# Layer 0 of a two-layer transformer: ScalarE in the order of the source, later sums of the experts' weights, and their last step as a stream of its own

## The chip, the cores and the metric

The kernel runs on one core of a Trainium2 chip. The metric is the device time of one execution in microseconds (us); the time of a kernel is the median of several executions. The engines are TensorE (PE: matmuls, with PEld its weight loads), VectorE (DVE), ScalarE (ACT), GpSimd (POOL) and SyncE (SP, which here only issues DMAs).

## The reference, cut to what matters

Two layers, each of attention and a feed-forward part, each with a layer norm ahead of it and added to a residual, on 4 sequences of 512 rows of width 256. All is in float32.

```python
x = x + _L0_attn_ref(_layernorm(x), w_project, w_out)      # 16 heads of 16, causal, softmax over keys
x = x + _L0_ffn_ref(_layernorm(x), router_w, router_b, expert_w, expert_b)
x = x + _L1_attn_ref(_layernorm(x), w_qkv, w_proj)
x = x + _L1_ffn_ref(_layernorm(x), gate..., up..., down...)  # 4-bit weights

# _L0_ffn_ref: for every row and every one of 256 outputs a router over 8 experts
logits = (h @ router_w.T + router_b).reshape(T, O, E)
probs = softmax(logits, axis=-1)
w, sel = top_k(probs, 2)
w = w / sum(w, axis=-1)
c = zeros((T, E)).at[t_idx, sel].add(w)          # an expert's weights summed over the outputs
expert_out = einsum('th,eoh->teo', h, expert_w) + expert_b
final = einsum('te,teo->to', c, expert_out)
```

So each row has 256 x 8 logits; from each eight the two greatest are taken, their normalised weights are `sigmoid` of their gap and one minus it, and for each of the 8 experts these are summed over the 256 outputs. The change lies in how and when these sums are made.

## The kernel before

The residual stays in SBUF as 16 row tiles of 128 rows (`xres`), in 4 blocks of 4 tiles. Layer 0's attention runs over 44 batches (`batches`): a block j, a sequence s, and one to four groups of heads. For batch n the loop does, in this order:

1. `greatest(n + 1)`: first scores of the next batch (L631), in four PSUM tiles of the pool `l0_sc`, which has five; `shift(n)`: a transpose of the maxima (L660) and their subtraction from the queries by VectorE (L663); `mask(n + 1)` (L644), and VectorE's maxima of the first scores (L650, four operations).
2. A fill: pieces of other work, up to a budget of TensorE and VectorE time.
3. `mixed(n - 1)`: powers times values (L715, copied by ScalarE at L723); `powers(n)`: second scores (L679) in four tiles of the same five, then four exps on ScalarE (L688) and a causal select on POOL (L698).
4. A second fill.

As first and second scores share five PSUM banks, `powers(n)` needs banks that the maxima of batch n + 1 have read, and `greatest(n + 2)` needs banks that the exps of batch n have read.

What a fill gives out is cut into pieces by generators, each in a `Stream`: a piece tells which engine's budget it takes, how much, after how many slots, and on what condition. A slot is one call of `fill`; outside the waiting loops at a block's end there are two in a batch. The streams are asked in the order of the list `streams`. Layer 0's feed-forward part runs wholly in such streams, about half of it in the fills of layer 1's attention (`between`):

- `logit_pieces`: router products (L226, `lg_ps`), copied by ScalarE to `lg` (L289); tile g is allowed when `g - 2 in weights`.
- `weight_pieces`: for each row tile, on VectorE, the two greatest of eight (L363 to L378), then `lesser` on ScalarE (a tanh, L382, and L383, deferred by two slots), the logits less the second greatest (L389), and for each expert two accumulations. One is on VectorE (`junk`, L413). The other is `sum_up` on ScalarE (L406): the sum of `relu(-owing)` over the outputs, where `owing` is a running VectorE tile (L400, L416). Last, two small operations (L419, L420) turn sums into weights `c1`, and `weights[g]` tells that they are there.
- `result_pieces`: expert products (L226, `eo`), scaled by ScalarE with `c1` (L315, `part`); `addition_pieces` adds them to the residual (L342 to L344).
- `made()` counts the steps of `weight_pieces`, 17 for each tile, and paces products.

An operation put off with `defer` is issued at the start of the first fill that is at least one slot later (or as many as asked):

```python
for due in [d for d in deferred if d[0] <= slot]:
    deferred.remove(due)
    due[1]()
```

The projections of the attention's next block (`project`) are copied by ScalarE to `stage`, a tile with one buffer (L533); eight DMAs issued by SP (L539) spread each half to `qk`, and the copy for the next half waits for them to land. All products of a fill, and the transposes and outputs of `divided` (`av_T`, `oq_T`, whose copy `aT` is L753, and `o`, L762), share the PSUM pool `dn` with two buffers.

The order of the instructions on an engine is either that of the source, for the engines named in `manual_schedule`, or chosen by the framework when the program is built, with operations under `high_priority` preferred. In layer 0 TensorE, VectorE and POOL are in the order of the source and ScalarE is not; layer 1 adds ScalarE.

Of the kernel before, what the change touches and what calls it, by code (L numbers as in the profile page):

```python
# [8 lines left out]
F32 = mybir.dt.float32  # L9
# [3 lines left out]
ALU = mybir.AluOpType  # L13
# [3 lines left out]
P = 128  # L17
HID = 256
NS, NB = 4, 512
NT = 16  # L20
# [5 lines left out]
NE = 8  # L26
# [6 lines left out]
def tile_transformer(  # L33
# [19 lines left out]
    nc = tc.nc  # L53
# [11 lines left out]
    for t, eng in ((0, nc.sync), (2, nc.scalar)):  # L65
        eng.dma_start(out=xres[:, t : t + 2, :], in_=x[:, t : t + 2, :])
    in_order = ctx.enter_context(ExitStack())
    order = {mybir.EngineType.PE, mybir.EngineType.DVE, mybir.EngineType.Pool}
    in_order.enter_context(tc.manual_schedule(engines=order))
    ident = const.tile([P, P], F32, name="ident")  # L70
    make_identity(nc, ident)
# [26 lines left out]
    w_ffn0 = ctx.enter_context(ExitStack())  # L98
# [2 lines left out]
    ew = wa.tile([P, 2, NE, HID], F32, name="ew")  # L101
    b1 = w_ffn0.enter_context(tc.tile_pool(name="f0_1", bufs=1, side="right"))
    b2 = w_ffn0.enter_context(tc.tile_pool(name="f0_2", bufs=2, side="right"))
    b5 = w_ffn0.enter_context(tc.tile_pool(name="f0_5", bufs=5, side="right"))

# [1 line left out]
    slot = 0  # L109

    def need(engine, cost, gap=0, cond=None):
        return engine, cost, gap, cond
# [18 lines left out]
    streams = []  # L131
    deferred = []

    def defer(emit, slots=1):

        deferred.append((slot + slots, emit))

    left = {"PE": 0.0, "DVE": 0.0}

    def fill(**budget):  # L140

        nonlocal slot
        slot += 1
        for due in [d for d in deferred if d[0] <= slot]:
            deferred.remove(due)
            due[1]()
        for engine, b in budget.items():
            left[engine] = min(left[engine], 0.0) + b
        again = True
        while again:  # L150
            again = False
            for stream in list(streams):
                while stream.ready(left):
                    engine, cost = stream.go()
                    left[engine] -= cost
                    again = True
                if stream.next is None:
                    streams.remove(stream)

    normed = []  # L160

# [91 lines left out]
    logits, weights, halves = {}, {}, {}  # L253
# [20 lines left out]
    def logit_pieces():  # L274

        nonlocal products_left
        for g in range(NT):
            for pair in range(4):
                yield need(
                    "PE", 1.85,  # L280
                    cond=lambda g=g, pair=pair, at=(g - 0.9 + 0.22 * pair if g > 1 else 0.0):
                    g // 4 in xTs and (0, pair) in folded and (g < 2 or g - 2 in weights) and made() >= at,
                )
                if not pair:
                    lg = b2.tile([P, NE, HID], F32, tag="lg", name=f"lg{g}")
                ps = ps_dn.tile([P, 512], F32, tag="dn", name=f"lg_ps{g}_{pair}")
                dense(ps, g, rw, pair)
                products_left -= 1
                nc.scalar.copy(  # L289
                    lg[:, 2 * pair : 2 * pair + 2, :].rearrange("p e o -> p (e o)"), ps  # L290
                )
            logits[g] = lg, slot
# [32 lines left out]
    def counted(pieces):  # L325
        nonlocal steps_made
        for piece in pieces:
            yield piece
            steps_made += 1
# [3 lines left out]
    def addition_pieces():  # L333
        for g in range(NT):
            for half in range(2):
                yield need(
                    "DVE", 1.55,
                    cond=lambda k=(g, half): k in halves and halves[k][1] < slot,
                )
                part = halves[g, half][0]  # L340
                tt = nc.vector.tensor_tensor
                tt(part[:, 0:2], part[:, 0:2], part[:, 2:4], ALU.add)  # L342
                tt(part[:, 0], part[:, 0], part[:, 1], ALU.add)
                tt(xres[:, g, :], xres[:, g, :], part[:, 0], ALU.add)  # L344
                added[g, half] = slot

    def weight_pieces():

        tt, stt = nc.vector.tensor_tensor, nc.vector.scalar_tensor_tensor
        lessers = []  # L350
        for g in range(NT):
            yield need("DVE", 1.25, cond=lambda: g in logits and logits[g][1] < slot)
            d = logits[g][0]
            hi4 = b1.tile([P, 4, HID], F32, tag="hi4", name=f"hi4_{g}")
            lo4 = b1.tile([P, 4, HID], F32, tag="lo4", name=f"lo4_{g}")
            m2 = b1.tile([P, HID], F32, tag="m2", name=f"m2_{g}")
            gap = b1.tile([P, HID], F32, tag="gap", name=f"gap_{g}")
            th = b1.tile([P, HID], F32, tag="th", name=f"th_{g}")
            w1 = b1.tile([P, HID], F32, tag="w1", name=f"w1_{g}")
            c1 = b2.tile([P, NE], F32, tag="c1", name=f"c1_{g}")  # L360
            sums = b2.tile([P, NE + 1], F32, tag="sums", name=f"sums_{g}")

            tt(hi4, d[:, 0:4], d[:, 4:8], ALU.max)  # L363
            yield need("DVE", 1.25)
            tt(lo4, d[:, 0:4], d[:, 4:8], ALU.min)
            yield need("DVE", 1.4)
            lo2, hi2 = lo4[:, 0:2], lo4[:, 2:4]
            tt(lo2, lo2, lo4[:, 2:4], ALU.max)
            tt(hi2, hi4[:, 0:2], hi4[:, 2:4], ALU.max)
            yield need("DVE", 1.4)  # L370
            tt(hi4[:, 0:2], hi4[:, 0:2], hi4[:, 2:4], ALU.min)
            tt(lo2, lo2, hi4[:, 0:2], ALU.max)
            yield need("DVE", 1.7)
            tt(gap, hi2[:, 0], hi2[:, 1], ALU.min)
            tt(m2, lo2[:, 0], lo2[:, 1], ALU.max)
            tt(m2, m2, gap, ALU.max)
            tt(gap, hi2[:, 0], hi2[:, 1], ALU.max)
            tt(gap, gap, m2, ALU.subtract)  # L378


            def lesser(th=th, gap=gap, w1=w1):
                nc.scalar.activation(th, gap, AF.Tanh, scale=0.5)  # L382
                nc.scalar.activation(w1, th, AF.Identity, bias=half_t, scale=0.5)  # L383
                lessers.append(th)

            defer(lesser, 2)
            for e in (0, 4):
                yield need("DVE", 1.25)
                tt(  # L389
                    d[:, e : e + 4], d[:, e : e + 4],  # L390
                    m2.unsqueeze(1).to_broadcast([P, 4, HID]), ALU.subtract,
                )

            yield need("DVE", 0.7, 1, cond=lambda: lessers)
            lessers.clear()
            owing = b5.tile([P, HID], F32, tag="owing", name=f"owing_{g}_")
            nc.vector.tensor_scalar(gap, gap, 0.0, -1.0, ALU.is_equal, ALU.mult)
            stt(owing, th, -1.0, gap, ALU.add, ALU.add)  # L400
            nc.vector.memset(sums[:, NE : NE + 1], 0.0)
            for e in range(NE):

                def sum_up(e=e, owing=owing, sums=sums, g=g):
                    spare = b2.tile([P, HID], BF16, tag="spare", name=f"spare_{g}_{e}")
                    nc.scalar.activation(  # L406
                        spare, owing, AF.Relu, scale=-1.0, accum_out=sums[:, e : e + 1]
                    )

                defer(sum_up)  # L410
                yield need("DVE", 0.95, cond=lambda: len(deferred) < 4)
                junk = b2.tile([P, HID], BF16, tag="junk", name=f"junk_{g}_{e}")
                stt(junk, d[:, e], 0.0, w1, ALU.is_gt, ALU.mult, accum_out=c1[:, e : e + 1])  # L413
                if e < NE - 1:
                    less = b5.tile([P, HID], F32, tag="owing", name=f"owing_{g}_{e}")
                    stt(less, d[:, e], 0.0, owing, ALU.is_equal, ALU.add)  # L416
                    owing = less
            yield need("DVE", 0.3, 1)
            tt(sums[:, :NE], sums[:, :NE], sums[:, 1:], ALU.subtract)  # L419
            stt(c1, sums[:, :NE], 0.5, c1, ALU.mult, ALU.add)  # L420
            weights[g] = c1, slot
            del logits[g]

    normed_first = []

# [7 lines left out]
    with ExitStack() as l0:  # L433
# [293 lines left out]
        def divided(j, s):  # L727
# [29 lines left out]
            for t in (0, 2):  # L757
# [12 lines left out]
                    yield need("DVE", 0.7, 1)  # L770
                both = xres[:, 4 * j + t : 4 * j + t + 2, :]
                nc.vector.tensor_tensor(both, both, ps, ALU.add)
            fold_at = streams.index(fold) if fold in streams else len(streams) - 4
            streams.insert(fold_at if j else 0, Stream(hidden_pieces(j)))


# [24 lines left out]
        for piece in inputs_T(1, both[1][0], xT):  # L801
# [4 lines left out]
        done = blanked = 0  # L806
        fold = Stream(fold_pieces())
        streams += [
            inputs[1], fold, Stream(addition_pieces()), Stream(counted(weight_pieces())),
            Stream(result_pieces()), Stream(logit_pieces()),  # L810
        ]
        for n in range(NBT):
            j, s, gs = batches[n]
# [90 lines left out]


    with ExitStack() as l1:
        in_order.enter_context(tc.manual_schedule(engines={mybir.EngineType.Activation}))
        wb = l1.enter_context(tc.tile_pool(name="w_l1", bufs=1))
        wqkv = wb.tile([P, 2, NKV, HPK + 2, P], F32, name="wqkv")

# [376 lines left out]
```

## Time and profile before

| what | value |
|---|---|
| median of 3 executions | 1183.99 us (1183.14 to 1185.19) |
| the profiled execution | 1185.96 us, of which the span 1184.2 us |
| mean granted clock of TensorE | 0.995 of full speed |
| TensorE busy | 1153.4 us, 97% of the span |
| VectorE busy | 807.9 us, 68% |
| ScalarE busy | 485.2 us, 41% |
| POOL busy | 106.4 us, 9% |
| layer 0's attention | to about 400 us of the span |
| last expert product of layer 0's feed-forward part | at 738 us, in layer 1's attention |

How to read the views: a row of a timeline has the start, the duration, the engine, the line of the kernel, the operation, what it writes and reads, the shape, and how many instructions were merged (`x4`); in brackets stand the idle time of the engine ahead of it and what ended that. A row of the waits has who waited, for whom, the microseconds in total, how often, and the longest. A row of the windows has a stretch of the span, its length, the busy time of PE, PEld, DVE, ACT and POOL with their numbers of instructions, the granted clock, the DMA share and GB/s.

### The profile page before, as it was taken

What the parts mean: (1) busy time and instruction counts of PE and PEld (TensorE: products, weight loads), DVE (VectorE), ACT (ScalarE), POOL (GpSimd) and SP (SyncE); (2) the same over time, 40 slices, a digit from 0 to 9 for tenths busy, and PEclk for the clock granted to TensorE, in tenths of its full rate; (3) what the DMA queues carried; (4) which work ended last, traced back from release to release, by engine and by line L of the source; (5) the groups of instructions that cost most, each with busy time, mean ns of one, the idle gap of its engine ahead of it and who ended that gap; (6) DMA issues with size and microseconds to landing.
All of it is one profiled execution on the core that took longest, in us unless ns stands there. A gap on an engine that the chain in (4) does not pass through costs nothing.

```text
span 1184.2 us, 18603 instructions
## 1 busy us (share of the span) xinstructions
PE 1153.4 (97%) x7178; PEld 666.0 (56%) x7178; DVE 807.9 (68%) x1783; ACT 485.2 (41%) x1099; POOL 106.4 (9%) x152
## 2 busy tenths in 40 slices
PE   7999999999999899999999999999999999999998
PEld 3666555555555445555555556566644465475487
DVE  5676779889889777368646783888599844725710
ACT  1434545555466444445344542455244322303300
POOL 7322112112111000000000000000000000000000
PEclk9999999999999999999999999999999999999999
DMA  7230010000000310000000001021010000000000
GB/s 216 66 79 2 16 22 1 2 1 1 2 1 2 117 62 1 1 1 1 1 1 1 1 7 31 18 65 26 18 52 4 0 1 18 0 1 18 1 12 24
DMA packets 21240, 26.46 MB, mean 22 GB/s; under 512 B 5128, under 2 KB 14600, under 8 KB 21152
## 3 DMA queue, kind: packets, MB, share of 16 engines
q1 hardware_dynamic: 20480, 24.10, 7.4%
q10 hardware_dynamic: 672, 1.18, 0.4%
q8 instruction: 56, 0.92, 0.3%
q14 instruction: 32, 0.26, 0.1%
HBM read 18.97 MB, written 2.10 MB: 18 GB/s over the span
## 4 chain that ended last, share of the span: by engine, by line
PE 82%; DVE 11%; ACT 2%; issue 2%; POOL 1%; DMA 1%; SPq 0%; ACTq 0%; DVEq 0%; POOLq 0%
PE qk_ps L967 11%; PE o L1058 10%; PE y L1214 9%; PE g L895 9%; PE u L895 9%; PE lg_ps L226 8%; PE eo L226 8%; PE s L631 4%; PE s L679 3%; DVE mx L650 3%; PE av L715 2%; PE v_ps L949 2%; PE qk_ps L529 2%; PE a L1038 1%; PE s L980 1%
## 5 line engine op out<-in xcount | busy, mean ns | idle before, releaser
L967 PE MATMUL qk_ps<-xT,wqkv 128*128 128x512 f32 x320 | 148.6, 598 | 0.3 <-ACT qT L971 0.3
L226 PE MATMUL lg_ps<-rw,xT 128*128 128x512 f32 x256 | 123.6, 607 | 3.9 <-ACT xT L934 1.6
L226 PE MATMUL eo<-ew,xT 128*128 128x512 f32 x256 | 122.4, 601 | 3.2 <-ACT part L315 1.0
L1058 PE MATMUL o<-wpj,oT 128*128 128x256 f32 x512 | 119.8, 382 | 0.0
L1214 PE MATMUL y<-wd,it 128*128 128x256 f32 x512 | 111.8, 379 | 0.0
L1058 PEld LDWEIGHTS o<-wpj,oT 128*128 128x128 f32 x512 | 95.7, 190 | 27.7 <-issue 15.1
L1214 PEld LDWEIGHTS y<-wd,it 128*128 128x128 f32 x512 | 97.0, 190 | 15.0 <-issue 2.2
L650 DVE TENSOR_REDUCE mx<-s 128x1 f32<-128x384 f32 (+3 forms) x176 | 100.5, 633 | 1.4 <-PE s L644 1.4
L967 PEld LDWEIGHTS qk_ps<-xT,wqkv 128*128 128x128 f32 x320 | 59.4, 190 | 68.7 <-issue 59.6
L688 ACT ACTIVATE pt<-s 128x512 f32<-128x512 f32 (+1 forms) x176 | 83.7, 560 | 23.4 <-PE s L679 23.4
L895 PE MATMUL g<-xT,wgu 128*128 128x512 f32 x192 | 90.4, 593 | 0.0
L895 PE MATMUL u<-xT,wgu 128*128 128x512 f32 x192 | 90.2, 592 | 0.0
L315 ACT ACTIVATE part<-eo,c 128x256 f32<-128x256 f32 x128 | 53.8, 472 | 86.5 <-PE eo L226 85.0
L698 POOL TENSOR_SCALAR_AFFINE_SELECT pt<-pt 128x256 f32<-128x256 f32 (+2 forms) x88 | 60.7, 696 | 266.5 <-ACT pt L688 265.8
L1192 ACT ACTIVATE th<-sq 128x512 f32<-128x512 f32 x64 | 40.3, 630 | 87.8 <-DVE sq L1191 87.8
L226 PEld LDWEIGHTS eo<-ew,xT 128*128 128x128 f32 x256 | 46.4, 191 | 49.0 <-issue 37.4
L226 PEld LDWEIGHTS lg_ps<-rw,xT 128*128 128x128 f32 x256 | 46.3, 191 | 49.2 <-issue 36.8
L214 DVE TENSOR_TENSOR xres<-xres,y 128x256 f32<-128x256 f32 x16 | 6.7, 421 | 92.2 <-PE y L1214 92.2
L177 POOL TENSOR_TENSOR ln_rs<-rs_v,minus_half 128x4 f32<-128x4 f32 x16 | 18.0, 1124 | 553.2 <-DVE rs_v L176 455.6
L631 PE MATMUL s<-qk 32*128 32x128 f32 (+3 forms) x512 | 62.2, 465 | 1.2 <-ACT pt L688 0.9
L1193 DVE SCALAR_TENSOR_TENSOR th<-th,g 128x512 f32<-128x512 f32 x63 | 43.2, 686 | 29.2 <-ACT th L1192 29.2
L289 ACT COPY lg<-lg_ps 128x512 f32<-128x512 f32 x64 | 37.6, 587 | 62.1 <-PE lg_ps L226 61.9
(233 smaller groups left out, 1763.2 us busy)
## 6 DMA issues: line engine op xcount, KB each, us to landing
qk<-stage SPq DMA_DIRECT2D x56, 64.0 KB, 2.4
wqkv<-in_w_qkv SPq DMA_DIRECT2D x8, 320.0 KB, 7.4
rw<-in_router_w SPq DMA_DIRECT2D x8, 256.0 KB, 7.5
ew<-in_expert_w SPq DMA_DIRECT2D x8, 256.0 KB, 4.6
wpj<-in_w_proj SPq DMA_DIRECT2D x1, 2048.0 KB
out<-xres SPq DMA_DIRECT2D x4, 512.0 KB, 2.6
xres<-in_x SPq DMA_DIRECT2D x3, 512.0 KB, 9.1
dq_wgu<-in_gate_w SPq DMA_DIRECT2D x8, 128.0 KB, 2.4
```

Source lines behind the costliest of these rows:

```text
L226: nc.tensor.matmul(ps, lhsT=xT[:, hc, (g % 4) * P : (g % 4 + 1) * P], rhs=w[:, hc, 2 * pair : 2 * pair + 2, :].rearrange("p e o -> p (e o) ...
L315: nc.scalar.mul(part[:, e % 4], ps[:, i], c[:, e : e + 1])
L631: nc.tensor.matmul(tiles[h][:, b * nk : (b + 1) * nk].rearrange("p (c k) -> p c k", k=P), lhsT=queries(j, g)[r, s], rhs=qk[r, g, : j + 1, ...
L650: nc.vector.tensor_reduce(maxes[n % 2][:, h, gs[0] : gs[0] + nb], ps[:, : nb * nk].rearrange("p (b k) -> p b k", b=nb), AX.X, ALU.max,)
L688: nc.scalar.activation(pt[:, i, : nb * nk], tiles[2 * pair + i][:, : nb * nk], AF.Exp, scale=0.25)
L698: nc.gpsimd.affine_select(out=last, in_=last, compare_op=ALU.is_ge, fill=0.0, base=0, pattern=pattern, channel_multiplier=-1,)
L895: nc.tensor.matmul(ps, lhsT=wgu[:, w, half, jj, par * P : (par + 1) * P], rhs=xT[:, half, :], start=half == 0, stop=half == 1,)
L967: nc.tensor.matmul(ps, lhsT=wqkv[:, hc, kv, h, :], rhs=xT[:, hc, :], start=hc == 0, stop=hc == 1,)
L1058: nc.tensor.matmul(ys[t // 2][:, t % 2], lhsT=state["o"][:, h, t * P : (t + 1) * P], rhs=wpj[:, HPK * kv + h, :], start=kv == 0 and h == 0 ...
L1192: nc.scalar.activation(th, sq, AF.Tanh, scale=0.7978845608028654)
L1193: nc.vector.scalar_tensor_tensor(th, th, 1.0, gp, ALU.add, ALU.mult)
L1214: nc.tensor.matmul(ps, lhsT=it[:, c // 2, c % 2, t * P : (t + 1) * P], rhs=wd[:, c // 2, c % 2, :], start=c == 0, stop=c == 2 * NJ - 1,)
```

## The change

ScalarE joins the engines that keep the order of the source from the start of the kernel, and the line that added it in layer 1 goes. `defer` takes a flag `last`; what is deferred with it is issued at the end of a fill rather than at its start. A `sum_up` deferred in a slot with an odd number (outside the waiting loops, the fill ahead of a batch's powers) gets that flag, so that it is issued at the end of the next fill; one deferred in an even slot is issued at the start of the next. More may be outstanding (six for four), and the pool that holds `owing` has eight buffers for five; `c1` and `sums` move to it from a pool with two. The last two operations of `weight_pieces` become `total_pieces`, a stream ahead of `weight_pieces`, which runs when all eight sums of a tile have been issued; `weight_pieces` goes on to its next tile without the one-slot gap that stood before them.

```diff
-    order = {mybir.EngineType.PE, mybir.EngineType.DVE, mybir.EngineType.Pool}
+    order = {
+        mybir.EngineType.PE, mybir.EngineType.DVE, mybir.EngineType.Pool,
+        mybir.EngineType.Activation,
+    }
...
-    b5 = w_ffn0.enter_context(tc.tile_pool(name="f0_5", bufs=5, side="right"))
+    b5 = w_ffn0.enter_context(tc.tile_pool(name="f0_5", bufs=8, side="right"))
...
-    def defer(emit, slots=1):
-
-        deferred.append((slot + slots, emit))
+    def defer(emit, slots=1, last=False):
+
+
+        deferred.append((slot + slots, emit, last))
+
+    def emit_deferred(last):
+        for due in [d for d in deferred if d[0] <= slot and d[2] == last]:
+            deferred.remove(due)
+            due[1]()
...
-        for due in [d for d in deferred if d[0] <= slot]:
-            deferred.remove(due)
-            due[1]()
+        emit_deferred(False)
...
                 if stream.next is None:
                     streams.remove(stream)
+        emit_deferred(True)
...
-            c1 = b2.tile([P, NE], F32, tag="c1", name=f"c1_{g}")
-            sums = b2.tile([P, NE + 1], F32, tag="sums", name=f"sums_{g}")
+            c1 = b5.tile([P, NE], F32, tag="c1", name=f"c1_{g}")
+            sums = b5.tile([P, NE + 1], F32, tag="sums", name=f"sums_{g}")
...
+            summed_up[g] = [c1, sums, 0]
             for e in range(NE):
 
                 def sum_up(e=e, owing=owing, sums=sums, g=g):
...
-                defer(sum_up)
-                yield need("DVE", 0.95, cond=lambda: len(deferred) < 4)
+                    summed_up[g][2] += 1
+
+                defer(sum_up, last=slot % 2 == 1)
+                yield need("DVE", 0.95, cond=lambda: len(deferred) < 6)
...
-            yield need("DVE", 0.3, 1)
-            tt(sums[:, :NE], sums[:, :NE], sums[:, 1:], ALU.subtract)
-            stt(c1, sums[:, :NE], 0.5, c1, ALU.mult, ALU.add)
+            del logits[g]
+
+    summed_up = {}
+
+    def total_pieces():
+        for g in range(NT):
+            yield need("DVE", 0.3, cond=lambda: g in summed_up and g not in logits and summed_up[g][2] == NE)
+            c1, sums, _ = summed_up.pop(g)
+            nc.vector.tensor_tensor(sums[:, :NE], sums[:, :NE], sums[:, 1:], ALU.subtract)
+            nc.vector.scalar_tensor_tensor(c1, sums[:, :NE], 0.5, c1, ALU.mult, ALU.add)
             weights[g] = c1, slot
-            del logits[g]
...
-            inputs[1], fold, Stream(addition_pieces()), Stream(counted(weight_pieces())),
-            Stream(result_pieces()), Stream(logit_pieces()),
+            inputs[1], fold, Stream(addition_pieces()), Stream(counted(total_pieces())),
+            Stream(counted(weight_pieces())), Stream(result_pieces()), Stream(logit_pieces()),
...
     with ExitStack() as l1:
-        in_order.enter_context(tc.manual_schedule(engines={mybir.EngineType.Activation}))
```

## The prediction

> **What bounds the kernel now.** I read the page first, then the waits by who waited for whom, then the timeline of TensorE beside that of ScalarE in layer 0. The page:
>
> ```profile
> span 1184.2 us, 18603 instructions
> PE 1153.4 (97%) x7178; PEld 666.0 (56%) x7178; DVE 807.9 (68%) x1783; ACT 485.2 (41%) x1099; POOL 106.4 (9%) x152
> PE 82%; DVE 11%; ACT 2%; issue 2%; POOL 1%; DMA 1%; SPq 0%; ACTq 0%; DVEq 0%; POOLq 0%
> ```
>
> TensorE is the bound, ScalarE has 59% of its time free. Its 485 us can't matter by their amount, only by lateness: where TensorE waits for one ScalarE result. But "97% busy" hides such waits, because a matmul that waits inside its group counts as busy. The waits of 128 to 390 us show them on the weight loads:
>
> ```profile
> ACT spare L406 <- DVE owing L416: 12.9, 20, 2.1
> ACT th L382 <- DVE gap L378: 11.1, 7, 2.3
> PEld s L631 <- ACT pt L688: 6.1, 13, 1.4
> ```
>
> Read upwards, these are one story. The next batch's first scores (L631) wait for exps (L688), which free their PSUM banks; and ScalarE in front of those exps sits waiting for VectorE, on a sum (L406) or a tanh (L382) that came too early in its queue. In TensorE's timeline:
>
> ```profile
> 283.64 1.14 PE L631 MATMUL s<-qk 32*128 32x512 f32 x8
> ...
> 291.30 1.12 PE L631 MATMUL s<-qk 32*128 32x512 f32 x2
> 292.62 2.10 PE L631 MATMUL s<-qk 32*128 32x512 f32 x6 [0.20 <-ACT pt L688]
> ...
> 325.56 3.22 PE L631 MATMUL s<-qk 32*128 32x512 f32 x8
> ```
>
> Eight of these matmuls take 1.14 us when nothing is late, 3.22 at 325.56. ScalarE before those two places:
>
> ```profile
> 290.15 0.42 ACT L406 ACTIVATE spare<-owing 128x256 bf16<-128x256 f32 x1 [1.77 <-DVE owing L416]
> ...
> 291.99 2.04 ACT L688 ACTIVATE pt<-s 128x512 f32<-128x512 f32 x4
> ...
> 325.19 0.42 ACT L382 ACTIVATE th<-gap 128x256 f32<-128x256 f32 x1 [2.31 <-DVE gap L378]
> ...
> 326.06 2.04 ACT L688 ACTIVATE pt<-s 128x512 f32<-128x512 f32 x4
> ```
>
> The second scores end at 289.46 and 323.73, so the exps start 2.5 and 2.3 us late.
>
> **Part 1: sums and tanh behind the exps (gain).** In source order a sum deferred in the fill before the powers comes at the end of the fill after them; one deferred in the fill after them comes at the start of the next fill, and waits only for VectorE work that stands ahead of the subtraction (L663) which the next second scores need. Either way it can't be what the exps wait for. The tanh, deferred by two slots, comes a whole batch after its subtraction L378. So each stretch that a sum or tanh caused should go. From the timeline's L631 rows, against 0.93 us (128x384 or narrower, the row at 145.97) and 1.14 (128x512):
> 135.28: 2.67-0.93 = 1.74 (tanh). 226.68: no product stands in that fill, so it waits anyway; the sum's share is the exps' start, 227.71 instead of 226.86, 0.85. 244.57: 2.38-0.93 = 1.45 (tanh). 261.43: 1.48-1.14 = 0.34 (sums). 291.30 to the transpose at 294.65: 3.35-1.07 = 2.28 (sums). 325.56: 2.08 (tanh). 335.39: 1.64-1.14 = 0.50 (sums). Together 9.2 us. Where exps were late but a product filled the time (185 and 219 us) I count nothing.
>
> Not all of it comes back, since VectorE is close behind:
>
> ```profile
> 128.80:376.10 247.30, 240.07 (x2445) 129.94 (x2441) 211.06 (x511) 134.22 (x367) 42.63 (x65) 0.98 0.03 6
> ```
>
> The fourth number pair is VectorE: 211.06 of 247.30 us, 85%, would be 89% of 238.1. During the stall at 292 it caught up; without the stall the maxima (L650, four in 2.48 us) come later for the second scores, which need their banks. It is late already at 288 and 363 us, where L679 takes 1.48 and 1.7 instead of 1.17 us. Bounds: 0 (all turned into waits for VectorE) to 9.2; I take three quarters, because in most batches of this stretch the second scores run at full speed today: **-6.9 us**.
>
> **Part 2: the clock (gain, uncertain).** Three stretches of 3.41 us run at half clock, one of them here:
>
> ```profile
> 227.36:230.77 3.41, 2.66 (x14) 1.56 (x14) 1.44 (x7) 2.36 (x8) 0.82 (x2) 1.00 0.00 0
> 230.77:234.18 3.41, 3.41 (x20) 1.35 (x22) 3.38 (x8) 0.59 (x1) 0.00 (x0) 0.50 0.00 0
> ```
>
> The third number from the end is the granted clock. The others begin at 138.61 and 247.84. Each costs half its length, 1.7 us, 5.1 in all, and each begins within 1 us of the end of a stretched L631 group that the change should mend. The Trainium skill, "TensorE: Matmul & The Clock Gate", section "Part 1: The HAM clock gate", speaks against counting on this: the clock falls after an idle window of about 3.4 us, and here the window before shows TensorE 2.66 of 3.41 us busy, the other two 3.40 and 3.25. By that rule these stretches are not the stalls' doing and stay: 0. By the rows' coincidence: -5.1. The longer stretches at 292 and 325 us drew no fall, so I take a third: **-1.7 us**.
>
> **Part 3: ScalarE can no longer step round a waiting copy (loss).** Taking every copy of layer 0 in the order of its matmuls, the queue of before departs from the source, sums and tanh aside, in two places, both `stage` copies of a second half (L533). The first:
>
> ```profile
> 73.53 2.06 ACT L688 ACTIVATE pt<-s 128x512 f32<-128x512 f32 x4 [0.53 <-PE s L679]
> 78.00 0.37 ACT L753 COPY aT<-oq_T 128x256 f32<-128x256 f32 x1 [2.41 <-PE oq_T L750]
> 79.94 1.09 ACT L533 COPY stage<-qk_ps 128x512 f32<-128x512 f32 x2 [1.57 <-DMA qk<-stage]
> ```
>
> ```profile
> 73.88 1.88 PE L529 MATMUL qk_ps<-xT,wp 128*128 128x512 f32 x4
> 77.59 0.38 PE L750 MATMUL oq_T<-ident,oq 128*128 128x128 f32 x2
> 78.43 1.98 PE L529 MATMUL qk_ps<-xT,wp 128*128 128x512 f32 x4 [0.46 <-ACT aT L753]
> ```
>
> `stage` has one buffer. The copy of the projection that ended at 75.76 waits for the eight SP transfers of the first half, to 79.94; meanwhile `aT` goes ahead and frees the PSUM buffer for the projection at 78.43. In source order `aT` stands behind, and both `dn` buffers stay held until 80.5: that projection starts 2.0 us later, and all of TensorE's order behind it. SP's eight second-half transfers follow by as much; SP has nothing behind them, and their block is read only after 130 us. POOL's selects (L698) follow their exps and lose nothing. Bounds: 0 to +2.3 (were the buffer freed by `aT` at 80.8); I take **+2.0 us**. The second place (144 to 154 us) is the same: the copy waits to about 150 for transfers issued from 142.35, and the projection at 148.06 would start at about 150.2. But there TensorE waits 2.25 us today at 153.97 for just this copy, and that wait goes: 0 net (-0.5 to +0.5).
>
> **Part 4: the last step its own stream, and eight buffers.** No instruction is added; the same two small VectorE operations (0.16 and 0.17 us) run once per row tile, up to one slot later. Cover: the products wait for them, but the next tile's maxima need not any more, so VectorE work of layer 1 moves into layer 0, and products with it. Layer 1 has TensorE at 100% from 500 to 600 us, so products move between the layers at no gain. The later sums can meet, two groups of three, on ScalarE; in layer 1 that is up to 2.4 us (0.40 each, back to back) ahead of a copy for which TensorE has 1.7 us of matmuls. TensorE's waits for ScalarE there are about 0.5 us today. 0 to +3, -1 where a fill that stood empty gets a product; I take 0, the nearest row being today's.
>
> **The sum.** -6.9 - 1.7 + 2.0 = -6.6 us on the profiled execution, which took 1185.96 us (span 1184.2 and 1.8 around it): 1179.4. It lay 2.0 above the median of 1183.99, so 1177.4 for the median.
>
> **The rivals.** (a) *VectorE takes the stall over.* For it: 85% busy, and its late maxima. Against: it idles 36 us of that stretch. With part 1 at 2 us, no clock gain and +2.0: about 1184, no change; with 3 to 4 us, 1182.
> (b) *Slower: head-of-line waiting on the `stage` transfers.* Place: the two copies. Price: 2.0 and 2.1 us with the old wait at 153.97 kept in another form, and a half-clock stretch after each, 3.4: +7.5. With parts 1 and 2 kept to 3 us: +4.5, 1188.5. It decides once parts 1 and 2 bring under 5 us. Against: both places have only about 2 us each and longer stalls drew no half clock.
> (c) *More than forecast.* All of 9.2 and 5.1 and 1 for filled slots, less 2.0: -13.3, 1170.7.
> (d) *The change doesn't do what it says*: if exps still wait for something in front, the sums at the start of a fill, L631 stays stretched; then +2, 1186. Against: the order of VectorE's work, as in part 1.
>
> **How the numbers follow.** A measurement of this kernel tells about 0.2%, 2.4 us, from no change: 1181.6 to 1186.4. Forecast (1172 to 1181.5): 0.58. (c): 0.11. (a) and (d), mostly within 0.2%: 0.14. (b): 0.17. Faster 0.69, same 0.14, slower 0.17. For 8 in 10 the range leaves out the bottom of (c) and the upper half of (b): 1169.5 to 1187.5.
>
> **What would show it.** Right: no L406 or L382 row between the second scores and their exps; L631 never over 1.6 us behind a filled slot; "ACT spare <- DVE owing" near zero in layer 0; `stage` then `aT` near 80 us, with TensorE waiting 2 us at its projection. Wrong: L679 waiting for L650 by more than before, half-clock stretches at new places, or TensorE under 99% in layer 1. Part 4 is wrong if products wait for the late sums and fills stand empty.

## The result, and the profile after

| | before | after |
|---|---|---|
| median of 11 executions | 1184.13 us (1181.25 to 1185.84) | 1179.94 us (1177.55 to 1182.32) |
| ratio to before | | 0.9964, 95% interval 0.9953 to 0.9975 |
| profiled span | 1184.2 us | 1180.3 us |

The change makes the kernel 4.2 us faster; 6.6 were predicted. A later measurement of the same kernel, beside other executions of before, gave 6.6 (below: it scatters by 5 us, and why). The page of after:

```profile
span 1180.3 us, 18580 instructions
PE 1148.1 (97%) x7178; PEld 663.9 (56%) x7178; DVE 809.7 (69%) x1783; ACT 484.3 (41%) x1099; POOL 108.1 (9%) x152
PE 79%; DVE 15%; ACT 2%; issue 2%; POOL 1%; DMA 1%; SPq 0%; ACTq 0%; DVEq 0%; POOLq 0%
```

TensorE is still the bound; its share of the chain that ends last went from 82 to 79%, VectorE's from 11 to 15. The waits of 128 to 390 us (lines have moved: L406 is L415 now, L382 is L390, L631 is L647, L688 is L704, L663 is L679, L533 is L549, L529 is L545):

```profile
PEld av L731 <- DVE qk L679: 8.1, 11, 1.5
ACT stage L549 <- DMA qk<-stage: 4.7, 1, 4.7
PEld s L647 <- ACT pt L704: 2.4, 6, 0.6
ACT spare L415 <- DVE owing L426: 0.7, 3, 0.3
ACT th L390 <- DVE gap L386: 0.3, 1, 0.3
```

The two rows that the prediction began with, 12.9 and 11.1 us of ScalarE waiting with a sum or tanh, are 0.7 and 0.3, and the wait of the first scores for the exps fell from 6.1 to 2.4. Two others rose. A `stage` copy waits 4.7 us, and powers times values wait 8.1 us for VectorE's subtraction from the queries, where the waits of before had:

```profile
PEld av L715 <- DVE qk L663: 5.2, 10, 0.8
```

TensorE's timeline, and under it ScalarE's:

```profile
293.87 1.14 PE L647 MATMUL s<-qk 32*128 32x512 f32 x8
...
324.22 1.14 PE L647 MATMUL s<-qk 32*128 32x512 f32 x8
...
330.75 2.12 PE L647 MATMUL s<-qk 32*128 32x512 f32 x8
```

```profile
322.45 2.07 ACT L704 ACTIVATE pt<-s 128x512 f32<-128x512 f32 x4 [0.85 <-PE s L695]
324.38 0.44 ACT L390 ACTIVATE th<-gap 128x256 f32<-128x256 f32 x1
...
330.12 2.07 ACT L704 ACTIVATE pt<-s 128x512 f32<-128x512 f32 x4 [1.16 <-PE s L695]
```

The tanh stands behind its exps, and the exps wait only for TensorE's second scores, never for something of their own queue. That holds for all 32 groups of exps between 128 and 376 us; before, 14 of 31 stood behind a sum or a tanh. The eight first scores take 1.14 us where 3.22 stood before at 325.56, and behind a product they never take over 1.25 us. Six groups of them still take 1.6 to 2.7, the 2.12 at 330.75 among them. These are no late exps: their slots hold nothing or only transposes, too little to cover the exps' own 1.64 or 2.07 us. This is part 1 as predicted.

Now the `stage` copies. ScalarE and TensorE near 78 us:

```profile
72.93 2.06 ACT L704 ACTIVATE pt<-s 128x512 f32<-128x512 f32 x4 [0.53 <-PE s L695]
79.57 0.59 ACT L549 COPY stage<-qk_ps 128x512 f32<-128x512 f32 x1 [4.58 <-DMA qk<-stage]
80.05 0.38 ACT L769 COPY aT<-oq_T 128x256 f32<-128x256 f32 x1
```

```profile
76.98 0.38 PE L766 MATMUL oq_T<-ident,oq 128*128 128x128 f32 x2
80.21 3.78 PE L545 MATMUL qk_ps<-xT,wp 128*128 128x512 f32 x4 [2.85 <-ACT stage L549]
```

and near 150 us, TensorE and ScalarE:

```profile
151.73 3.78 PE L545 MATMUL qk_ps<-xT,wp 128*128 128x512 f32 x4 [3.20 <-ACT stage L549]
```

```profile
151.09 0.59 ACT L549 COPY stage<-qk_ps 128x512 f32<-128x512 f32 x1 [4.71 <-DMA qk<-stage]
```

ScalarE stands 4.6 and 4.7 us with a copy whose tile the DMAs still read, `aT` stands behind it, and TensorE stands still for about 3 us. In the brackets the idle time is only half the price: the four projections take 3.78 us instead of 1.88. The windows show why (the third number from the end is the granted clock):

```profile
76.03:79.45 3.42, 1.33 (x15) 0.72 (x10) 3.37 (x7) 0.00 (x0) 0.29 (x1) 1.00 0.47 79
79.45:86.28 6.83, 6.07 (x41) 2.78 (x41) 1.39 (x3) 1.45 (x3) 0.00 (x0) 0.50 0.04 7
```

```profile
147.71:151.13 3.42, 0.82 (x11) 0.53 (x7) 3.42 (x12) 0.04 (x1) 0.00 (x0) 1.00 0.45 74
151.13:157.95 6.82, 6.22 (x48) 3.23 (x52) 1.12 (x6) 4.05 (x16) 0.00 (x0) 0.50 0.06 9
```

After each stall TensorE runs at half clock for 6.83 us. These are the only half-clock stretches of this profile between its start and its last matmul; the three of before are gone.

Laid side by side by the start of each batch's transpose of the maxima (L660 before, L676 after; batches counted from 0), after minus before: batches 0 to 5 -0.6, batch 6 +4.3, batch 11 +4.3, batch 13 +0.9, batch 14 +4.3, batch 42, the last but one, -3.5, the end of the span -3.9. So the first `stage` stall cost 4.9, the second 3.4, and the stretches between and behind, to batch 42, gained 3.4 and 7.8. The gain is 11.2, the loss 8.3.

### The profile page after: what moved, and what is told of

The parts are those of the page before. It is cut to its first block, busy times and chain, and to the rows that moved or that the text cites. A ratio compares the mean times of both kernels' runs of the same rounds, so it can differ in the third digit from the quotient of the medians.

```text
span 1180.3 us, 18580 instructions
## 1 busy us (share of the span) xinstructions
PE 1148.1 (97%) x7178; PEld 663.9 (56%) x7178; DVE 809.7 (69%) x1783; ACT 484.3 (41%) x1099; POOL 108.1 (9%) x152
## 4 chain that ended last, share of the span: by engine, by line
PE 79%; DVE 15%; ACT 2%; issue 2%; POOL 1%; DMA 1%; SPq 0%; ACTq 0%; DVEq 0%; POOLq 0%
PE qk_ps L982 11%; PE y L1229 9%; PE o L1073 9%; PE g L911 9%; PE u L911 9%; PE lg_ps L234 8%; PE eo L234 7%; DVE mx L666 3%; PE s L647 3%; PE s L695 3%; PE av L731 2%; PE qk_ps L545 2%; PE v_ps L964 2%; PE a L1053 1%; PE s L995 1%
## 5 line engine op out<-in xcount | busy, mean ns | idle before, releaser
L704 ACT ACTIVATE pt<-s 128x512 f32<-128x512 f32 (+1 forms) x176 | 84.1, 564 | 36.3 <-PE s L695 36.3
L911 PEld LDWEIGHTS u<-xT,wgu 128*128 128x128 f32 x192 | 36.5, 190 | 45.9 <-issue 44.7
```

Source lines behind the costliest of these rows:

```text
L704: nc.scalar.activation(pt[:, i, : nb * nk], tiles[2 * pair + i][:, : nb * nk], AF.Exp, scale=0.25)
L911: nc.tensor.matmul(ps, lhsT=wgu[:, w, half, jj, par * P : (par + 1) * P], rhs=xT[:, half, :], start=half == 0, stop=half == 1,)
```

## The experiments

Theory S: order of the source and late sums bring what was predicted, and the `stage` stalls eat most of it. Rival V: VectorE took the gain over, and stalls cost little. All ratios are to executions of before on the same chip.

**A free tile for the second halves (e1_after_free_stage, e2_before_free_stage).** For the two waiting halves, `stage` is another tile that is idle then, so the copies need not wait for the transfers:

```diff
-                if j or half:
+                if j == 2 and half:
+                    stage = unused("stage2_1", "p (i q) -> p i q", i=2)
+                elif j == 3 and half:
+                    stage = b1.tile([P, 4, HID], F32, tag="part", name="stage3_1")
+                    stage = stage.rearrange("p (i a) o -> p i (a o)", i=2)
+                elif j or half:
```

> The changed kernel, but the second half's copies of blocks 2 and 3 go to buffers that are free then (one of lg, one of part), so that ScalarE waits for no transfer at the two stage copies. Theory S (each stage copy at the head of ScalarE's queue stalls TensorE by about 3 us and then brings half clock): both waits and both half-clock stretches go, 4.9 + 3.4 us, so about 1171.5 (1170 to 1174). Rival V (VectorE is the bound of layer 0 by now, and takes most of it): 1176 to 1179. Rival C (the half clock has nothing to do with the stalls): half-clock stretches stay somewhere, about 1175.

Measured: 1170.58 us (1169.84 to 1170.99), ratio 0.9878 (0.9865 to 0.9891). TensorE, then ScalarE:

```profile
77.77 0.38 PE L771 MATMUL oq_T<-ident,oq 128*128 128x128 f32 x2
77.99 1.88 PE L545 MATMUL qk_ps<-xT,wp 128*128 128x512 f32 x4
```

```profile
75.98 0.59 ACT L549 COPY stage<-qk_ps 128x512 f32<-128x512 f32 x1 [0.20 <-PE qk_ps L545]
78.19 0.37 ACT L774 COPY aT<-oq_T 128x256 f32<-128x256 f32 x1 [1.62 <-PE oq_T L771]
```

Both stalls are gone, no half-clock stretch is left between the start and the last matmul, all four executions have a granted clock of 1.0, and the change is worth 14.5 us. Theory S stands: 9.4 us were lost to two copies (7.6 if the second median of the change is taken, 1178.15, below).

The same edit on the kernel before (e2_before_free_stage):

> The kernel before, with the same two other buffers for the stage copies. Theory S: only the waits that stood there go, 2.25 us at 154 and 0.46 + 0.17 at 78, so 1181 to 1182; the exps that were late behind sums and the three half-clock stretches stay. Rival: the planner's order moves and nothing is gained or something is lost, 1184 to 1186.

Measured: 1179.42 us (1177.68 to 1181.07), ratio 0.9951 (0.9939 to 0.9964), 5.6 us faster, more than expected. Its profile has one half-clock stretch (at 224.86 us) where before has three. At a granted clock of 1.0 two of its executions took 1177.7 us, and the six of before on all chips 1181.3 to 1183.0. So 3.5 us or more of the 5.6 are not clock; the prediction's rows show waits of 0.46 and 2.25 for the two copies, and where the rest of it comes from is open. Neither of the two half-clock stretches that went lay behind a `stage` copy: presumably a shift of a few us against the clock's windows (below) was enough.

**Which part of the change carries the gain (e3_order_only, e4_sums_only).** The kernel before with the order alone:

```diff
-    order = {mybir.EngineType.PE, mybir.EngineType.DVE, mybir.EngineType.Pool}
+    order = {
+        mybir.EngineType.PE, mybir.EngineType.DVE, mybir.EngineType.Pool,
+        mybir.EngineType.Activation,
+    }
...
-        in_order.enter_context(tc.manual_schedule(engines={mybir.EngineType.Activation}))
```

> The kernel before with ScalarE in the order of the source in layer 0 and nothing else: sums are issued at the start of the next fill, four outstanding, the last step inside weight_pieces. Theory O (the order alone frees the exps, since a sum at a fill's start is behind the exps or needs only VectorE work ahead of the next subtraction): the same gain of about 11 us and the same loss of about 8 at the stage copies, 1180 to 1183. Rival L (the later sums carry the gain: at a fill's start they make ScalarE wait for VectorE, and the copies behind it are late): 1186 to 1192.

Measured: 1178.74 us (1176.02 to 1180.49), ratio 0.9945 (0.993 to 0.9959). The order alone brings what the change brings, and 1.3 us more than Theory O's range allowed. In its trace, too, all 32 groups of exps between 128 and 376 us wait only for their scores, and both stalls are there:

```profile
80.25 1.98 PE L532 MATMUL qk_ps<-xT,wp 128*128 128x512 f32 x4 [3.15 <-ACT stage L536]
...
148.88 1.98 PE L532 MATMUL qk_ps<-xT,wp 128*128 128x512 f32 x4 [3.17 <-ACT stage L536]
```

And the kernel after with this same edit undone, so all the rest without the order:

> The change without its first part: sums later, six outstanding, eight buffers, the last step its own stream, but ScalarE's order in layer 0 left to the planner. Theory O: the planner goes on putting sums and tanh ahead of exps, no stage wait is added; 1182 to 1185. Rival L (the later place in the source is enough): exps on time without the stage waits, 1173 to 1176.

Measured: 1189.2 us (1186.6 to 1191.25), ratio 1.0037 (1.0023 to 1.005): slower, which neither theory expected. From its waits of 128 to 390 us:

```profile
PEld s L644 <- ACT pt L701: 9.5, 23, 1.7
ACT th L387 <- DVE gap L383: 9.0, 6, 2.3
ACT spare L412 <- DVE owing L423: 8.1, 15, 2.1
```

Where ScalarE's order is not that of the source, it doesn't help that the source issues the sums later: 16 of 31 groups of exps still stand behind a sum or a tanh, and TensorE's next first scores wait 9.5 us for exps (6.1 before). Its profile also has four half-clock stretches (199, 230, 329 and 363 us), 17.1 us in all, where the three of before have 10.2; half of the difference, 3.4 us, is lost by that alone.

**The half clock (e5_after_again, e6_after_spin).** The order-only kernel has the same stalls as the change and no half clock in its profile. That led to theory H: the fall follows from TensorE standing still, and whether it comes depends on how the stall lies against windows of 3.41 us that run freely. Two things in the profiles speak for such windows: every half-clock stretch ahead of the last matmul is 3.41 or 6.83 us long and begins a whole number of them after the first change of the clock, and that first change comes at another time in each profile, 10.67 to 13.23 us into the span. The windows, counted in steps of 3.413 from the first change of the clock in the order-only trace (10.67 us), cut its first stall in two:

```profile
75.52:78.93 3.41, 1.58 (x22) 0.95 (x15) 3.36 (x7) 0.00 (x0) 0.54 (x1) 1.00 0.57 94
78.93:82.35 3.42, 2.10 (x5) 0.78 (x5) 0.37 (x1) 0.94 (x3) 0.00 (x0) 1.00 0.00 0
```

TensorE is busy for 1.58 and 2.10 us of them, where it was 1.33 and 0.82 in the windows ahead of the falls in the profile of after. To test it, the change was run again as it is, and with three idle matmuls that run while TensorE would stand still:

```diff
+            if j > 1 and half and i:
+                spin = ps_mm.tile([P, 512], F32, tag="mm", name=f"spin{j}")
+                for k in range(3):
+                    nc.tensor.matmul(
+                        spin, lhsT=ident, rhs=wp[:, 0, :512], start=not k, stop=k == 2
+                    )
```

> The changed kernel once more, to stand beside the next one on the same chip: 1178 to 1182, with a spread of some 4 us from run to run, if half-clock stretches after its two stage waits come in some executions and not in others.

> The changed kernel with three more 128x512 matmuls (of ident and wp, into the bank of mxT, read by nobody; 2.6 us of TensorE) just ahead of each projection that waits about 3 us for a stage copy. Theory H (the half clock follows from TensorE standing still in the stall): the waits stay, the half clock goes; 1176 to 1178, a spread under 2.5 us, lower than the changed kernel by 2 to 4. Rival N (half clock comes from something else): the same or up to 5 us more than the changed kernel, with half-clock stretches still there.

Measured: the change again 1178.15 us (1175.12 to 1180.18), ratio 0.9953 (0.9935 to 0.9972), with a half-clock stretch of 3.41 us at 80.58, behind the first stall, and one at 200.05, which is behind neither, in its profile; with the idle matmuls 1175.73 us (1175.04 to 1176.27), 0.3 below what was expected, ratio 0.9931 (0.9918 to 0.9945), no half clock, a spread of 1.2 us instead of 5. The first stall of the change run again lies in the first of the windows below; its second, no shorter (2.95 us for 2.52), is cut in two by 148.85 and drew no half clock:

```profile
77.17:80.58 3.41, 0.89 (x7) 0.61 (x7) 3.04 (x6) 0.63 (x2) 0.00 (x0) 1.00 0.35 58
145.43:148.85 3.42, 2.28 (x17) 0.84 (x15) 3.38 (x13) 0.13 (x1) 0.41 (x1) 1.00 0.59 98
148.85:152.26 3.41, 1.59 (x4) 0.68 (x4) 2.59 (x10) 2.23 (x10) 0.00 (x0) 1.00 0.07 11
```

The half clock at 200.05 begins at the end of a stretched group of first scores, which take 0.93 us when nothing is late:

```profile
197.89 2.15 PE L647 MATMUL s<-qk 32*128 32x384 f32 x7
```

TensorE and ScalarE with the idle matmuls:

```profile
77.44 2.84 PE L545 MATMUL spin<-wp,ident 128*128 128x512 f32 x6
80.31 1.98 PE L551 MATMUL qk_ps<-xT,wp 128*128 128x512 f32 x4
```

```profile
79.67 0.58 ACT L555 COPY stage<-qk_ps 128x512 f32<-128x512 f32 x1 [4.46 <-DMA qk<-stage]
```

The copy waits as long as ever and the projection starts as late, but at full clock. More work on TensorE makes the kernel 2.4 us faster, and its time steady: the granted clocks of its six executions are 0.999 or 1.0, those of the change run again 0.994 to 1.0. Theory H stands. So of the 7.6 to 9.4 us that free tiles bring, 5.2 are the standing still itself (1175.73 less the 1170.58 with free tiles), and the rest, 2.4 to 4.2 by the two medians of the change, is clock. The one execution of the change at a granted clock of 1.0 agrees: 1175.12.

**The later sums and their own stream (e7 to e11).** All these have the free tiles. First the order alone, that is, the edit of e3 and that of the free tiles on the kernel before:

> The order of the source and the free buffers for stage, with sums at the start of the next fill, four outstanding, the last step inside weight_pieces: what the rest of the change is worth with no stage wait to disturb it. Theory O (order and stage are all): 1170 to 1172, as e1. Rival L (the later sums and the stream of their own bring a part): 1173 to 1177.

Measured: 1170.38 us (1170.15 to 1170.93), ratio 0.9887 (0.987 to 0.9903), the same as with the whole change. And the whole change, but with the last step back in `weight_pieces`:

```diff
+            yield need("DVE", 0.3, 1, cond=lambda: summed_up[g][2] == NE)
+            tt(sums[:, :NE], sums[:, :NE], sums[:, 1:], ALU.subtract)
+            stt(c1, sums[:, :NE], 0.5, c1, ALU.mult, ALU.add)
+            weights[g] = c1, slot
...
-            inputs[1], fold, Stream(addition_pieces()), Stream(counted(total_pieces())),
-            Stream(counted(weight_pieces())), Stream(result_pieces()), Stream(logit_pieces()),
+            inputs[1], fold, Stream(addition_pieces()), Stream(counted(weight_pieces())), Stream(result_pieces()), Stream(logit_pieces()),
```

> As e1 (the change with free buffers for stage), but the last step of the weights is back inside weight_pieces with its gap of one slot; sums stay late. If the own stream is worth nothing: 1170 to 1172. If it is what lets VectorE go on without a gap and that counts: 1173 to 1176. If it costs (results a slot later): under 1169.5.

Measured: 1185.4 us (1183.96 to 1188.1), ratio 1.0009 (1.0002 to 1.0016), outside what was expected. Its profile loses time in a few places, most of them again ScalarE's queue. The largest, in layer 1, ScalarE and then TensorE:

```profile
441.82 0.42 ACT L415 ACTIVATE spare<-owing__4971 128x256 bf16<-128x256 f32 x1 [1.82 <-DVE sums L409]
...
444.34 1.05 ACT L957 COPY xT<-xT_ps 128x512 f32<-128x512 f32 x2
```

```profile
439.17 1.64 PE L210 MATMUL xT_ps<-ident,xn 128*128 128x128 f32 x8 [0.28 <-DVE xn L194]
444.96 3.78 PE L234 MATMUL lg_ps<-rw,xT 128*128 128x512 f32 x4 [4.15 <-ACT xT L957]
```

Four sums, the first of which waits for VectorE, stand ahead of the copy of a transposed norm; TensorE stands still for 4.15 us, and the half clock from 442.93 to 449.76 takes 3.4 more. Five sums ahead of such a copy at 394 us cost 1.8 of standing and 1.7 of clock (a stretch at 395.14), two waits at 385 to 388 us cost 2.4, and a stall at 745.73 us, behind a conversion as in the next run, 3.0 and 1.7. Together 18, against 15 in the result; the whole change has small waits of its own at such places.

The remaining corner of the square, early sums with the own stream:

```diff
-                defer(sum_up, last=slot % 2 == 1)
+                defer(sum_up)
```

> ScalarE in the order of the source, the last step its own stream, and the free stage tiles, but every sum comes at the start of a slot as in the kernel before (none a slot later). It is e1_after_free_stage without the late sums, and e7_order_free_stage with the own stream alone. e1 took 1170.6, e7 1170.4, e8 (late sums without the own stream) 1185.4. Theory A (the own stream is worth about 15 us by itself, and the late sums cost that): 1155 to 1160. Theory B (the own stream only undoes what the late sums cost, because with early sums the last step waits for nothing): 1169 to 1172, the same as e7. Theory C (e8's loss is an accident of its order around the start of layer 1, where a layer norm meets four sums on ScalarE, and such accidents of a few us come and go with any edit): anywhere from 1168 to 1178.

Measured: 1176.94 us (1173.9 to 1178.18), ratio 0.9933 (0.9917 to 0.995). Theories A and B both fail; the time lies in the range of C, which was wide. The place, VectorE, ScalarE and TensorE:

```profile
732.78 0.43 DVE L895 TENSOR_SCALAR dq_mgu<-dq_wgu 128x512 int32<-128x512 int32 x1 [2.82 <-DMA dq_wgu<-in_up_w]
```

```profile
733.66 1.15 ACT L897 ACTIVATE dq_bgu<-dq_mgu,minus 128x1024 f32<-128x1024 int32 x1 [4.50 <-DVE dq_mgu L896]
```

```profile
736.30 1.12 PE L210 MATMUL xT_ps<-ident,xn 128*128 128x128 f32 x4 [3.04 <-ACT qT L991]
```

VectorE's unpacking of layer 1's packed weights finds its load not yet there, ScalarE's conversion waits for VectorE, and TensorE for a `qT` copy behind the conversion. These loads are issued behind the last expert product, which ends at 725 us here, at 704 with the whole change; with the order alone it ends at 723 and no such wait follows, so it is a matter of which slots meet. Two runs put that unpacking later, by at least one slot for all four weights, and by five for the first:

```diff
-        yield need("DVE", 0.9)
+        yield need("DVE", 0.9, 1)
```

> e9_early_sums_own_stream (order, free stage, own stream, early sums; 1176.9), with one edit in layer 1: the unpacking of the gate and up weights starts one slot after its loads are issued, instead of in the slot that issues them (need("DVE", 0.9, 1) for need("DVE", 0.9) at its first step). In the profile of e9 VectorE waits 2.82 us at 732.78 for such a load, the conversion of ScalarE behind it 4.50, and TensorE stands still for 3.04 us at 736.30, and runs at half clock for the 6.8 us after (3.4 lost); the profiles of e1 and e7 have no such wait. Theory C (e9 is slower than e7 by that accident): the wait goes and the time falls by about 6.4 to 1170.5 (1169 to 1172.5), as e1 and e7. Theory B' (the own stream with early sums costs something throughout): the wait goes, but the time stays above 1174.

Measured: 1177.03 us (1174.74 to 1177.53), ratio 0.9921 (0.9906 to 0.9937). The edit moved too little: the wait of 2.81 us and the stall of 3.03 are still in the profile, so this run tells nothing apart.

> e9_early_sums_own_stream with the first unpacking of the gate and up weights in layer 1 five slots later (need("DVE", 0.9, 5) for the first of the four). In e10 one slot moved it too little: the wait of 2.81 us for the load was still there, and the time, 1177.0, that of e9. Here VectorE's unpacking stands behind the layer norm's xn, and ScalarE's conversion behind the copies of qT, oT and kT, which TensorE waits for. Theory C (e9 is slower than e7 by that accident): TensorE's stall of 3.04 us and its half clock go, time 1170.5 (1169 to 1173). Theory B' (the own stream with early sums costs something throughout): above 1174.

Measured: 1173.13 us (1171.24 to 1173.87), ratio 0.9897 (0.9882 to 0.9913). The wait for the load is 0.2 us, and TensorE goes on:

```profile
732.87 0.60 PE L210 MATMUL xT_ps<-ident,xn 128*128 128x128 f32 x4
```

3.8 of the 6.6 us between this corner and the order alone are that one stall. The time is 0.1 above the range of theory C. Its profiled execution, 1173.13 us, has a half-clock stretch from 168.59 to 175.41 us, worth 3.4, and e9 has one at 169.17. In the window ahead, TensorE stands still for VectorE, in a fill that is empty in this kernel:

```profile
166.95 0.86 PE L736 MATMUL av<-pt,va 128*32 128x128 f32 x24 [1.67 <-DVE qk L684]
```

and that has a product in the order alone (e7):

```profile
165.27 1.94 PE L229 MATMUL lg_ps<-rw,xT 128*128 128x512 f32 x4
167.13 0.86 PE L723 MATMUL av<-pt,va 128*32 128x128 f32 x24
```

The prediction had named empty fills as a sign against part 4; the whole change with free tiles has a product in this one. That this place makes the remaining 2.8 us was not tested.

## Why the prediction was right or wrong

**Right in kind, and in the range.** The predicted mechanism acted and the kernel is faster by over 0.2%; 1179.94 stands against 1177.4 (1169.5 to 1187.5). Taken by pairs of runs:

| step | predicted | measured | from |
|---|---|---|---|
| parts 1 and 2, order and clock | -8.6 | -9.0 | order alone to before, both with free tiles: 1170.38 - 1179.42 |
| part 3, `stage` copies, net of what they cost before | +2.0 | +3.8 (+2.0) | after less its free-tile version, 9.4 (7.6 with the second median), less the same of before, 5.6 |
| part 4, own stream, buffers, late sums | 0 | +0.2 | whole change to order alone, both with free tiles: 1170.58 - 1170.38 |
| sum | -6.6 | -5.0 (-6.8) | the change itself: -4.2, and -6.6 when measured again |

Not all of these pairs ran beside each other, so a figure is good to 1 or 1.5 us, and the last row lies within the scatter that the half clock makes. In the one profile of after both sides were larger than forecast, gains of 11.2 us for 8.6 and losses of 8.3 for 2.0. That the sum still came out near the forecast is in part luck.

**Part 1** was right: the stretches behind products went. The pair can't tell it from part 2, but the granted clocks can. Two executions of before with free tiles had a granted clock of 1.0 and took 1177.7 us, and all four of the order alone with free tiles had it and took 1170.4: 7.3 for part 1 (predicted: 6.9), and 1.7 for the clock. Rival (a) was a small part of it: VectorE is late more often (8.1 us for 5.2), but as waits of at most 1.5 us.

**Part 2** was put at a third of 5.1 us, between a row and a rule. That the pair gives just this 1.7 is luck, since the third was a weight between the two and not worked out; in the profile of after all three stretches are gone. The rule (the Trainium skill, "TensorE: Matmul & The Clock Gate", "Part 1: The HAM clock gate") asks for an idle window of about 3.4 us, and TensorE was never idle for a whole one. The measurement decides for the row: in the profile of after the clock falls behind windows with 1.33 and 0.82 us of busy TensorE, and filling the stall with matmuls takes the fall away. What the section says of a window that runs freely fits: the same kernel shows two stretches of 6.83 us in one profile, and 3.41 us at 80.58 in another.

**Part 3 is the step that was mis-sized**, in two terms, because the half clock behind each stall was left out of it. The first place was put at 2.0 us, "0 to +2.3", since the projection would start as much later; TensorE stood still for 2.85, and with the half clock behind it the place cost 4.9 in this profile. The second was put at "0 net", since an old wait of 2.25 us at 153.97 would go. It did go, but the new wait of 3.20 and the clock cost 3.4 more than it. How much the clock adds depends on the execution: the profiled one, 1182.05 us, is among the slowest of its eleven, and by the second median of the change part 3 comes to the +2.0 of the forecast, but from other terms: 5.2 of standing still and 2.4 of clock, less the 5.6 of before. Rival (b) had named just this, copies that wait for transfers and "a half-clock stretch after each", at 7.5; the profile shows 8.3. It was set aside because "longer stalls drew no half clock". That was no ground. The stalls at 292 and 325 us were stretched groups, and such groups drew half clock elsewhere: the three stretches of before, that at 224.86 us in e2 and all four in e4 begin inside one or within 1 us of its end. Whether a stall draws it depends on how it lies against the windows. So half-clock stretches at new places, a sign of being wrong that the prediction had named, did come. Rival (b) came out as a mechanism, and not as a sign, because parts 1 and 2 brought more than its limit of 5 us.

**Part 4** came out at nothing, but not for the reason given. Each of its halves alone costs: late sums with the last step in line 15 us, the own stream with early sums 6.6. At the places shown above, what changed is which copies meet a waiting instruction ahead of them on ScalarE, and which fills stand empty. That both together cost nothing is how the places fall in this kernel, and no cover that can be counted on.

**The best version.** The order of the source with free tiles for the second halves, and nothing else of the change, runs at 1170.38 us: 14.4 faster than before and 7.8 to 9.6 than the change.

## What to carry to other kernels

Before an engine is put into a written order, list on that engine the instructions that wait for a DMA, and ask what stands behind each: in a written order the price is what TensorE stands still for meanwhile, plus the loss of clock behind it. Here a second tile at two such places was worth more than all moving of the sums. And where a small edit shifts hundreds of instructions, compare all corners of it: a part's price alone (15 and 6.6 us here) may say only which accidental meetings it made.

## What the runs showed of the hardware

A stall of TensorE of about 3 us cost up to about twice its length here: half clock for 3.41 or 6.83 us followed (stalls of 2.85 and 3.20 us in the profile of after, 2.52 in e5), or nothing did (3.15 and 3.17 in e3, 2.95 in e5). In windows that hold most of such a stall, the clock fell after 1.33 us of busy time and less in 3.42 (1.33 and 0.82 in after, 0.89 in e5), and where a boundary cut the stall in two it did not, after 1.58 and 2.10 (e3), 2.28 and 1.59 (e5). The line between is not sharp: it fell after 1.49 in e10 (405.52 to 408.94 us) and after 1.75 in e11 (165.17 to 168.59), behind stalls of 1.94 and 1.67 us, and held after 1.41 at the end of e6 (1168.86 to 1172.27). The windows ahead of the falls of before show 2.66 us and more, but a stretched group counts as busy while it waits.

These windows lie differently in each execution (the first change of the clock is at 11.18 us in one profile of the change and at 12.31 in the other), so a kernel with such a stall scatters by 5 us (1175.1 to 1180.2), and one without, or with idle matmuls in the gap, by about 1 (1170.15 to 1170.93, 1175.04 to 1176.27). Executions of one kernel on one core whose granted clocks differ (0.994 to 1.0 in e5) were thus a sign that TensorE stood still, or waited inside a group, for 2 or 3 us somewhere.
